# Two graph layers on one core: PSUM banks of the first layer grouped by the engine that empties them

## The chip, the cores and the metric

The kernel runs on one core of one Trainium2 chip. The metric is device time in microseconds (us): the median of repeated executions. Before the change it is 2896.18 us (three runs, 2895.3 to 2902.11).

The engines are called here as the profile calls them: PE (TensorE, matrix products), PEld (its weight loads), DVE (VectorE), ACT (ScalarE), POOL (GpSimd), SP (SyncE, which starts transfers). PE writes its results into PSUM, eight banks of 512 fp32 values per partition. DVE or ACT takes a result up into the ordinary on-chip memory, and only then can PE fill that bank anew. Emptying a bank in this way is called taking it up.

## The reference, cut to what matters

Inputs are 16 graphs of 1024 nodes with 128 features each (`x`), a weighted adjacency `adj` of 16 x 1024 x 1024, and a node mask.

```python
# layer 0: three steps per graph
h = jnp.maximum(_layernorm(x), 0.0)
for i in range(3):
    h = h @ W[i] + b[i]
    nh = h / jnp.maximum(jnp.linalg.norm(h, axis=-1, keepdims=True), EPS)
    ew = edge_weight * jnp.einsum('bij,bkj->bik', nh, nh)
    h = jnp.einsum('bpq,bqc->bpc', ew, h)          # relu between steps
x = x + h

# layer 1
h = jnp.maximum(_layernorm(x), 0.0)
adj_d = adj * dilate(adj > 0, mask)                # row by row; each row's removals act on later rows
for i in (1, 2, 3):
    agg = adj_d @ h / clip(sum(adj_d), 1)
    h_i = batchnorm(relu(normalize(agg @ Wr + h @ Wx + b)))
x = x + (concat(h_1, h_2, h_3) @ Wl + bl)
```

`dilate` depends on `adj` and the mask alone, not on the features. The kernel can therefore work on it while layer 0 runs.

## The kernel before, in words

The program has two stages. The first (lines 169 to 775) holds layer 0 for all 16 graphs and, interleaved with it, the dilation. The second (from line 778) holds layer 1. The change touches the first stage only.

**Layer 0.** A graph's 1024 x 1024 matrix is treated as 8 x 8 blocks of 128 x 128. The cosine matrix is symmetric, so only the block rows q with their 8 - q blocks from the diagonal on are multiplied. Per graph and step (48 in all), and per block row, the methods of `Batch` do this:

- `products` (L296): PE multiplies up to four blocks at a time into a bank `pg` (L311). DVE multiplies it by the adjacency and writes both the block and the one that mirrors it into `ew` (L320 the diagonal block, L323 the others).
- `turn` (L331): the mirrored blocks are transposed by PE into a bank `gt` (L340), and ACT copies them back into `ew` (L341).
- `sums` (L343) and `sums_back` (L359): PE adds the blocks times the features into `po`, two banks that stay open for the whole step (L351, L365). At the end ACT takes `po` up as `hTo` (L374).
- `features` (L252), `turned` (L274), `scaled` (L280): the next step's features go through a bank `pw` (L260), which DVE takes up (L264 or L270). They are normalized and transposed through `pt_n` (helper `transposed`, L165 and L166, taken up by ACT).
- `adjT_tile` (L216): blocks of the adjacency are transposed through banks `pt_a` (L227), taken up by ACT (L228). `enter` transposes the entering features (`pt_h`). `residual` turns the result back through `px` (L385), taken up by DVE (L388).

`layer0` (L406) writes these steps out by hand as a generator. A block row's `sums` follow its `products` by three block rows (`LAG = 3`), the transposes come in between, and each `yield` returns a weight.

**Dilation.** `dilation` goes through 8 row blocks in two halves of 8 graphs each. For each graph it loads adjacency rows (`an`, L535) and kept entries (`kl`, L541), and ACT makes the pattern (`patt`, L537 and L538). PE then transposes it and makes thresholds (`pdt` L559, `pT` L566 to L568, both taken up by ACT). A few rounds follow, in which PE counts into a bank `pc` (L622, L623) and DVE computes the next estimate (L639, L593, L613, L617). A last transpose goes through `pe` (L671), taken up by ACT (L672). Then DVE scans each graph's rows (L689), ACT takes absolute values (L698), DVE compares (L709) and POOL stores (L710).

The loop at L744 advances layer 0 by the returned weights so that the two works go forward side by side. The dilation gets through when layer 0 has done 93% of its share (`SPREAD = 0.93`). After it comes a branch (L769) that holds an exact second dilation, which is run only if the quick one did not settle.

**Who sets the order.** The tile framework orders the instructions of each engine when the program is built. It goes by program order as priority, by the data, and by when a buffer of the right pool is free. On the chip each engine carries its own list out in that order. A tile gets a bank out of its pool's fixed number, so the number and the mixture of tiles in a pool enter into the order as well as into the waits.

The PSUM pools before are `a_sm` (2 banks: `pt_a`, `pt_h`, `pt_n`, `pw`, `px`, `pdt`, `pT`, `pc`, `pe`, `mt`, `pf`), `a_g` (2 banks: `pg`), `a_o` (`po`, one tile of 2 banks) and `a_t` (2 banks: `gt`).

Of the kernel before, what the change touches and what calls it, by code (L numbers as in the profile page):

```python
# [8 lines left out]
F32 = mybir.dt.float32  # L9
# [7 lines left out]
P = 128  # L17
# [29 lines left out]
def tile_adj_preln_d2(  # L47
# [112 lines left out]
    def transposed(psum_pool, dst, src, nm, func=AF.Copy, halves=range(NHALF)):  # L160

        for h in halves:
            pt = psum_pool.tile([P, CPH, P], F32, tag="sm", name=f"pt_{nm}_{h}")
            for c in range(CPH):
                nc.tensor.transpose(pt[:, c, :], src[:, h * CPH + c, :], ident)  # L165
            nc.scalar.activation(dst[:, h * CPH : (h + 1) * CPH, :], pt, func)  # L166


    with ExitStack() as actx:
        pool1 = actx.enter_context(tc.tile_pool(name="a1", bufs=1))  # L170
        pool2 = actx.enter_context(tc.tile_pool(name="a2", bufs=2))
        ps_sm = actx.enter_context(tc.tile_pool(name="a_sm", bufs=2, space=PSUM))
        ps_g = actx.enter_context(tc.tile_pool(name="a_g", bufs=2, space=PSUM))
        ps_o = actx.enter_context(tc.tile_pool(name="a_o", bufs=1, space=PSUM))
        ps_t = actx.enter_context(tc.tile_pool(name="a_t", bufs=2, space=PSUM))

        w0 = pool1.tile([P, 3, P], F32, name="w0")
        b0 = pool1.tile([P, 3, P], F32, name="b0")
# [37 lines left out]
        def adjT_tile(b, q):  # L216

            place, nat, row = adj_place(b, q), Nat.pop((b, q)), NCH - q
            if row > 1:
                nc.sync.dma_start(  # L220
                    place[:, row:, :].rearrange("p c q -> p (c q)"), adj[b][q * P : (q + 1) * P, (q + 1) * P :]
                )
            for c in range(0, row, CPH):
                n = min(CPH, row - c)
                pt = ps_sm.tile([P, CPH, P], F32, tag="sm", name=f"pt_a{b}_{q}_{c}")
                for i in range(n):
                    nc.tensor.transpose(pt[:, i, :], nat[:, c + i, :], ident)  # L227
                nc.scalar.activation(place[:, c : c + n, :], pt[:, :n, :], AF.Copy)  # L228
            nc.gpsimd.dma_start(adjT_d[b][q][:, q * P :], place[:, :row, :].rearrange("p c q -> p (c q)"))

        class Batch:
# [15 lines left out]
            def enter(self, h):  # L247
                if h == 0:
                    self.hT = pool2.tile([P, NCH, P], F32, tag="hT", name=f"hT_{self.b}")
                transposed(ps_sm, self.hT, self.h, f"h{self.b}", halves=(h,))  # L250

            def features(self, h):  # L252

                nm, l, rn = f"{self.b}_{self.l}", self.l, self.rn
                if h == 0:
                    self.hN = pool1.tile([P, NCH, D], F32, tag="hN", bufs=1, name=f"hN_{nm}")
                hc = slice(h * CPH, (h + 1) * CPH)
                pw = ps_sm.tile([P, CPH, P], F32, tag="sm", name=f"pw_{nm}_{h}")
                for c in range(CPH):
                    nc.tensor.matmul(  # L260
                        pw[:, c, :], lhsT=self.hT[:, h * CPH + c, :], rhs=w0[:, l, :], start=True, stop=True
                    )
                if rn is None:
                    nc.vector.tensor_tensor(  # L264
                        self.hN[:, hc, :], pw, b0[:, l : l + 1, :].to_broadcast([P, CPH, P]), ALU.add
                    )
                else:
                    for c in range(CPH):
                        n = h * CPH + c
                        nc.vector.scalar_tensor_tensor(  # L270
                            self.hN[:, n, :], pw[:, c, :], rn[:, n : n + 1], b0[:, l, :], ALU.mult, ALU.add
                        )

            def turned(self):  # L274

                nhT = pool1.tile([P, NCH, P], F32, tag="nhT", bufs=2, name=f"nhT_{self.b}_{self.l}")
                transposed(ps_sm, nhT, self.hN, f"n{self.b}_{self.l}")
                self.next_nhT = nhT.rearrange("p c q -> p (c q)")

            def scaled(self):  # L280
# [15 lines left out]
            def products(self, s):  # L296

                q = SEQ[s]  # L300
                nm = f"{self.b}_{self.l}_{q}"
                row = NCH - q

                most = max(NCH - SEQ[s % 4], NCH - SEQ[s % 4 + 4])
                ew = pool1.tile([P, 2 * most - 1, P], F32, tag=f"ew{s % 4}", name=f"ew_{nm}")
                place = adj_place(self.b, q)
                both = [t[:, 1 : 2 * row - 1, :].rearrange("p (t c) q -> p t c q", t=2) for t in (ew, place)] if row > 1 else None
                for c in range(0, row, CPH):
                    n = min(CPH, row - c)
                    pg = ps_g.tile([P, CPH, P], F32, tag="pg", name=f"pg_{nm}_{c}")  # L310
                    nc.tensor.matmul(  # L311
                        pg[:, :n, :].rearrange("p c q -> p (c q)"),
                        lhsT=self.nhT[:, q * P : (q + 1) * P],
                        rhs=self.nhT[:, (q + c) * P : (q + c + n) * P],
                        start=True,
                        stop=True,
                    )
                    own = c == 0
                    if own:
                        nc.vector.tensor_tensor(ew[:, 0, :], pg[:, 0, :], place[:, 0, :], ALU.mult)  # L320
                    if n > own:
                        off = slice(c + own - 1, c + n - 1)
                        nc.vector.tensor_tensor(  # L323
                            both[0][:, :, off, :],
                            pg[:, own:n, :].unsqueeze(1).to_broadcast([P, 2, n - own, P]),
                            both[1][:, :, off, :],
                            ALU.mult,
                        )
                return (ew,)

            def turn(self, s, ew):  # L331

                q = SEQ[s]
                row = NCH - q
                for c in range(1, row, CPH):
                    n = min(CPH, row - c)
                    pt = ps_t.tile([P, CPH, P], F32, tag="gt", name=f"gt_{self.b}_{self.l}_{q}_{c}")
                    at = row + c - 1
                    for i in range(n):
                        nc.tensor.transpose(pt[:, i, :], ew[:, at + i, :], ident)  # L340
                    nc.scalar.activation(ew[:, at : at + n, :], pt[:, :n, :], AF.Copy)  # L341
# [37 lines left out]
            def residual(self):  # L379
                b = self.b  # L380
                self.x2 = x2 = pool2.tile([P, NCH, D], F32, tag="tt", name=f"x2_{b}")
                for h in range(NHALF):
                    pt = ps_sm.tile([P, CPH, P], F32, tag="sm", name=f"px_{b}_{h}")
                    for c in range(CPH):
                        nc.tensor.transpose(pt[:, c, :], self.hT[:, h * CPH + c, :], ident)  # L385
                    for c in range(CPH):
                        n = h * CPH + c
                        nc.vector.scalar_tensor_tensor(  # L388
                            x2[:, n, :], pt[:, c, :], self.rn[:, n : n + 1], self.xb[:, n, :], ALU.mult, ALU.add
                        )  # L390
                nc.gpsimd.dma_start(x2_d[b].rearrange("(c p) d -> p c d", p=P), x2)
# [125 lines left out]
        def dilate(k, half, exact):  # L517
# [14 lines left out]
            for i in range(BH):  # L532
# [21 lines left out]
                if i % GT == GT - 1:  # L554
                    four = range(i - GT + 1, i + 1)
                    bs_ = slice(i - GT + 1, i + 1)
                    pdt = ps_sm.tile([P, GT, P], F16, tag="sm", name=f"pdt{nk}_{i}")
                    for n, ii in enumerate(four):
                        nc.tensor.transpose(pdt[:, n, :], pattern(ii)[:, diag], ident16)  # L559
                    dT = pool2.tile([P, GT, P], F16, tag="dT", bufs=1, name=f"dT{nk}_{i}")  # L560
                    nc.scalar.activation(dT, pdt, AF.Copy)
                    nc.vector.tensor_scalar(rbias[:, bs_], rest[:, bs_], 2.0, -2.0, ALU.mult, ALU.add)
                    yield 0.1
                    pT = ps_sm.tile([P, GT, P], F32, tag="sm", name=f"pT{nk}_{i}")
                    for n, ii in enumerate(four):
                        nc.tensor.matmul(pT[:, n, :], lhsT=dT[:, n, :], rhs=upto, start=True, stop=False)  # L566
                        nc.tensor.matmul(pT[:, n, :], lhsT=pattern(ii)[:, diag], rhs=off, start=False, stop=False)
# [28 lines left out]
            def removals(x, nm):  # L596
# [13 lines left out]
                else:  # L610
# [4 lines left out]
                        nc.vector.tensor_tensor(ev, ev, x, ALU.is_gt)  # L615
                        nc.vector.scalar_tensor_tensor(par, x, 1.0, ev, ALU.is_gt, ALU.mult)
                    nc.vector.tensor_tensor(E, T, mid.unsqueeze(2).to_broadcast([P, BH, P]), ALU.is_equal)  # L617
                pc = ps_sm.tile([P, BH], F32, tag="sm", name=f"pc_{nm}")
                for i in range(BH):
                    c = pc[:, i : i + 1]  # L620
                    if ends:
# [44 lines left out]
            if ends:  # L666
                nc.vector.tensor_tensor(Z, Z, par.unsqueeze(2).to_broadcast([P, BH, P]), ALU.mult)
                nc.vector.tensor_tensor(E, E, Z, ALU.add)
            pe_ = ps_sm.tile([P, BH, P], F16, tag="sm", name=f"pe{nk}")
            for i in range(BH):  # L670
                nc.tensor.transpose(pe_[:, i, :], E[:, i, :], ident16)  # L671
            nc.scalar.activation(E, pe_, AF.Copy)  # L672
# [59 lines left out]
        nc.gpsimd.dma_start(mi, nodemask.rearrange("b (c p) -> (b c) p", p=P))  # L732
        mfl = pool1.tile([P, P], F32, tag="up", name="mfl")[:NB, :]
        nc.vector.tensor_copy(mfl, mi)
        mt = ps_sm.tile([P, NB], F32, tag="sm", name="mt")
        nc.tensor.transpose(mt, mfl, ident[:NB, :NB])
        mf_flat = mf.rearrange("p b c -> p (b c)")
        nc.vector.tensor_copy(mf_flat, mt)
# [7 lines left out]
            while at * total < done * SPREAD * total0 and step0():  # L746
                pass

        pf = ps_sm.tile([1, B // 2], F32, tag="sm", name="pf")
        nc.tensor.matmul(pf, lhsT=ones_col, rhs=astray, start=True, stop=True)  # L750
        off_f = pool1.tile([1, 1], F32, name="off_f")
        nc.vector.tensor_reduce(off_f, pf, mybir.AxisListType.X, ALU.add)
# [382 lines left out]
```

## Time and profile before

| what | us |
|---|---|
| median of three runs | 2896.18 |
| the profiled execution, its own time | 2901.99 |
| its span from first to last instruction | 2900.3 |
| mean granted PE clock | 0.978 |
| PE busy in the span | 2667.8 |
| DVE busy | 1937.8 |
| ACT busy | 1426.8 |
| POOL busy | 467.5 |
| last dilation compare on DVE (L709) starts | 1578.3 |
| last `pg` product of layer 0 (L311) starts | 1694.9 |

The profile comes from one execution. Its own time is 5.8 us above the median of the runs. "Busy" counts a matmul from its start to its modelled end, and matmuls overlap, so a row of products shows as busy without a gap even though each of them takes up PE's entrance for less time than its own duration.

### The profile page before, as it was taken

To read this page: it belongs to the slowest core of one execution; us is meant where nothing else is said; L and a number is where in the kernel's file an instruction comes from. 1 tells how busy PE (TensorE), PEld (TensorE's weight loads), DVE (VectorE), ACT (ScalarE), POOL (GpSimd) and SP (SyncE) were. 2 spreads that over 40 slices of the span, in tenths; PEclk is the share of its full clock that TensorE was granted. 3 is DMA by queue.
4 is the path that set the end of the run, shared out by engine and by line. 5 is a ranking of instruction groups with operands and counts; after the bars stand their busy time and mean duration, and the time that the engine had idled before them with its cause. 6 is when DMAs were issued, how large, how long until landed. Compare 5 with 4: busy or idle time off the path is not lost. (4 is left out here: it accounts for less than half of the span.)

```text
span 2900.3 us, 52009 instructions
## 1 busy us (share of the span) xinstructions
PE 2667.8 (92%) x18803; PEld 2203.2 (76%) x18803; DVE 1937.8 (67%) x4913; ACT 1426.8 (49%) x4100; POOL 467.5 (16%) x619
## 2 busy tenths in 40 slices
PE   6999999899999998988999979999989999899997
PEld 4666676666666666666676758988979999899996
DVE  3787778877878788779877447777772232355565
ACT  6767667557556566455455323333333333333334
POOL 3111112011111111021011002222220010010101
PEclk9999999999999999999999989999999999999999
DMA  9446357347355475296162049999995656566764
GB/s 282 138 142 215 87 173 238 88 143 209 102 178 166 111 231 158 72 258 188 40 190 96 1 154 409 405 403 387 405 371 174 210 199 208 182 228 231 235 226 136
DMA packets 382236, 585.24 MB, mean 202 GB/s; under 512 B 85201, under 2 KB 266449, under 8 KB 381969
## 3 DMA queue, kind: packets, MB, share of 16 engines
q1 hardware_dynamic: 343280, 425.28, 46.4%
q0 software_dynamic: 38688, 156.53, 14.5%
q8 instruction: 152, 2.49, 0.3%
q14 instruction: 116, 0.94, 0.1%
HBM read 403.44 MB, written 163.58 MB: 196 GB/s over the span
## 5 line engine op out<-in xcount | busy, mean ns | idle before, releaser
L832 PE MATMUL agg<-hw,aT 128*128 128x128 f32 (+1 forms) x6144 | 744.8, 277 | 8.6 <-DVE aT L942 7.3
L832 PEld LDWEIGHTS agg<-hw,aT 128*128 128x128 f32 x6144 | 713.5, 193 | 14.3 <-DVE aT L942 9.7
L311 PE MATMUL pg<-nhT 128*128 128x512 f32 (+3 forms) x1152 | 454.0, 497 | 71.4 <-DVE ew L323 61.3
L351 PE MATMUL po<-ew,hS 128*128 128x512 f32 (+3 forms) x1152 | 455.5, 499 | 8.4 <-ACT hTo L374 4.3
L323 DVE TENSOR_TENSOR ew<-pg,adjA 128x768 f32<-128x768 f32 (+3 forms) x528 | 423.4, 824 | 3.7 <-DVEq L769 3.2
L365 PE MATMUL po<-ew,hS 128*128 128x128 f32 x2688 | 368.2, 277 | 0.0
L365 PEld LDWEIGHTS po<-ew,hS 128*128 128x128 f32 x2688 | 339.8, 193 | 35.5 <-issue 34.0
L341 ACT ACTIVATE ew<-gt 128x512 f32<-128x512 f32 (+1 forms) x480 | 208.7, 465 | 266.8 <-PE gt L340 262.7
L311 PEld LDWEIGHTS pg<-nhT 128*128 128x128 f32 x1152 | 188.8, 192 | 174.2 <-issue 131.3
L689 DVE TENSOR_TENSOR_SCAN rank<-patt 128x1024 f16<-128x1024 f16 x128 | 293.0, 2294 | 0.8
L351 PEld LDWEIGHTS po<-ew,hS 128*128 128x128 f32 x1152 | 195.7, 194 | 99.2 <-issue 68.7
L340 PEld LDWEIGHTS gt<-ident,ew 128*128 128x128 f32 x1344 | 169.6, 144 | 97.9 <-issue 71.1
L320 DVE TENSOR_TENSOR ew<-pg,adjA 128x128 f32<-128x128 f32 x384 | 107.2, 279 | 183.0 <-PE pg L311 143.2
L340 PE MATMUL gt<-ident,ew 128*128 128x128 f32 x1344 | 213.2, 278 | 3.5 <-ACT ew L341 3.2
L882 POOL TENSOR_TENSOR o<-o,rn 128x512 f32<-128x512 f32 x96 | 107.2, 1116 | 651.3 <-DVE rn L881 632.5
L804 PE MATMUL pw<-wrx,hT 128*128 128x256 f32 x768 | 182.4, 392 | 10.4 <-ACT hT L1007 9.7
L806 DVE TENSOR_TENSOR own<-pw,bs 128x256 f32<-128x256 f32 x192 | 81.3, 423 | 152.2 <-ACT hw L805 152.2
L804 PEld LDWEIGHTS pw<-wrx,hT 128*128 128x128 f32 x768 | 147.0, 197 | 33.5 <-ACT hT L1007 10.5
L960 ACT ACTIVATE aT<-pta 128x512 f32<-128x512 f32 (+3 forms) x160 | 71.2, 466 | 203.1 <-PE pta L959 172.2
L861 DVE SCALAR_TENSOR_TENSOR o<-agg,invdeg,own 128x128 f32<-128x128 f32 x384 | 109.7, 344 | 87.1 <-PE agg L832 78.4
L877 ACT ACTIVATE own<-o 128x128 f32<-128x128 f32 x384 | 114.6, 301 | 106.7 <-DVE o L861 106.7
L288 POOL TENSOR_TENSOR hS<-hN,rn 128x1024 f32<-128x1024 f32 x48 | 94.9, 1978 | 398.8 <-DVE rn L157 299.5
(165 smaller groups left out, 3950.1 us busy)
## 6 DMA issues: line engine op xcount, KB each, us to landing
an<-in_adj_dram SPq DMA_DIRECT2D x128, 512.0 KB, 4.7
keep<-kp POOLq DMA_DIRECT2D x128, 256.0 KB, 4.0
kb<-keep SPq DMA_DIRECT2D x128, 256.0 KB, 5.6
aT<-adT SPq DMA_DIRECT2D x32, 960.0 KB, 5.2
aT<-adT SPq DMA_DIRECT2D x32, 832.0 KB, 5.0
aT<-adT SPq DMA_DIRECT2D x32, 704.0 KB, 4.8
aT<-adT SPq DMA_DIRECT2D x32, 576.0 KB, 3.4
xb<-in_x_dram SPq DMA_DIRECT2D x31, 512.0 KB, 4.8
```

The lines of the kernel that those rows point to most:

```text
L311: nc.tensor.matmul(pg[:, :n, :].rearrange("p c q -> p (c q)"), lhsT=self.nhT[:, q * P : (q + 1) * P], rhs=self.nhT[:, (q + c) * P : (q + c ...
L320: nc.vector.tensor_tensor(ew[:, 0, :], pg[:, 0, :], place[:, 0, :], ALU.mult)
L323: nc.vector.tensor_tensor(both[0][:, :, off, :], pg[:, own:n, :].unsqueeze(1).to_broadcast([P, 2, n - own, P]), both[1][:, :, off, :], ALU ...
L340: nc.tensor.transpose(pt[:, i, :], ew[:, at + i, :], ident)
L341: nc.scalar.activation(ew[:, at : at + n, :], pt[:, :n, :], AF.Copy)
L351: nc.tensor.matmul(self.po[:, c * P : (c + n) * P], lhsT=self.hS[:, q, :], rhs=ew[:, c - q : c - q + n, :].rearrange("p c q -> p (c q)"), ...
L365: nc.tensor.matmul(self.po[:, q * P : (q + 1) * P], lhsT=self.hS[:, q + n, :], rhs=ew[:, NCH - 1 - q + n, :], start=False, stop=closes and ...
L689: nc.vector.tensor_tensor_scan(rank, pt[:, 1 : N + 1], pt[:, 2:], 0.0, ALU.add, ALU.add)
L804: nc.tensor.matmul(pw[:, i, :], lhsT=hT[:, 2 * h + i, :], rhs=wrx[:, l, :], start=True, stop=True)
L832: nc.tensor.matmul(self.place(c), lhsT=aT[:, blk, :], rhs=self.hw[:, source, :], start=source == 0 and c % self.ga == 0, stop=ends(c, source),
L861: nc.vector.scalar_tensor_tensor(self.o[:, c, :], self.place(c)[:, :P], invdeg[:, b, c : c + 1], self.own[:, c, :], ALU.mult, ALU.add,)
L877: nc.scalar.activation(self.own[:, n, :], self.o[:, n, :], AF.Square, accum_out=ss[:, c : c + 1])
```

## The change

Two pools of the first stage, `a_sm` and `a_t`, go away as such, and `a_g` too. In their place stand `a_v` with three banks for all tiles that DVE takes up (`pg`, `pw`, `px`, `pc`, `mt`, `pf`) and `a_s` with three banks for all tiles that ACT takes up (`pt_a`, `pt_h`, `pt_n`, `gt`, `pdt`, `pT`, `pe`). `po` keeps its two. No instruction is added or removed, and no size changes. All eight banks are in use before and after.

```diff
-        ps_sm = actx.enter_context(tc.tile_pool(name="a_sm", bufs=2, space=PSUM))
-        ps_g = actx.enter_context(tc.tile_pool(name="a_g", bufs=2, space=PSUM))
+
+        ps_v = actx.enter_context(tc.tile_pool(name="a_v", bufs=3, space=PSUM))
+        ps_s = actx.enter_context(tc.tile_pool(name="a_s", bufs=3, space=PSUM))
         ps_o = actx.enter_context(tc.tile_pool(name="a_o", bufs=1, space=PSUM))
-        ps_t = actx.enter_context(tc.tile_pool(name="a_t", bufs=2, space=PSUM))
...
-                pt = ps_sm.tile([P, CPH, P], F32, tag="sm", name=f"pt_a{b}_{q}_{c}")
+                pt = ps_s.tile([P, CPH, P], F32, tag="sm", name=f"pt_a{b}_{q}_{c}")
...
-                transposed(ps_sm, self.hT, self.h, f"h{self.b}", halves=(h,))
+                transposed(ps_s, self.hT, self.h, f"h{self.b}", halves=(h,))
...
-                pw = ps_sm.tile([P, CPH, P], F32, tag="sm", name=f"pw_{nm}_{h}")
+                pw = ps_v.tile([P, CPH, P], F32, tag="sm", name=f"pw_{nm}_{h}")
...
-                transposed(ps_sm, nhT, self.hN, f"n{self.b}_{self.l}")
+                transposed(ps_s, nhT, self.hN, f"n{self.b}_{self.l}")
...
-                    pg = ps_g.tile([P, CPH, P], F32, tag="pg", name=f"pg_{nm}_{c}")
+                    pg = ps_v.tile([P, CPH, P], F32, tag="sm", name=f"pg_{nm}_{c}")
...
-                    pt = ps_t.tile([P, CPH, P], F32, tag="gt", name=f"gt_{self.b}_{self.l}_{q}_{c}")
+                    pt = ps_s.tile([P, CPH, P], F32, tag="sm", name=f"gt_{self.b}_{self.l}_{q}_{c}")
...
-                    pt = ps_sm.tile([P, CPH, P], F32, tag="sm", name=f"px_{b}_{h}")
+                    pt = ps_v.tile([P, CPH, P], F32, tag="sm", name=f"px_{b}_{h}")
```

In the same way `pdt`, `pT` and `pe` go to `ps_s`, and `pc`, `mt` and `pf` to `ps_v`.

More of the change, by code (lines that the diff above doesn't have):

```diff
@@ L556, in dilate @@
                     bs_ = slice(i - GT + 1, i + 1)
-                    pdt = ps_sm.tile([P, GT, P], F16, tag="sm", name=f"pdt{nk}_{i}")
+                    pdt = ps_s.tile([P, GT, P], F16, tag="sm", name=f"pdt{nk}_{i}")
                     for n, ii in enumerate(four):
@@ L563, in dilate @@
                     yield 0.1
-                    pT = ps_sm.tile([P, GT, P], F32, tag="sm", name=f"pT{nk}_{i}")
+                    pT = ps_s.tile([P, GT, P], F32, tag="sm", name=f"pT{nk}_{i}")
                     for n, ii in enumerate(four):
@@ L617, in removals @@
                     nc.vector.tensor_tensor(E, T, mid.unsqueeze(2).to_broadcast([P, BH, P]), ALU.is_equal)
-                pc = ps_sm.tile([P, BH], F32, tag="sm", name=f"pc_{nm}")
+                pc = ps_v.tile([P, BH], F32, tag="sm", name=f"pc_{nm}")
                 for i in range(BH):
@@ L668, in dilate @@
                 nc.vector.tensor_tensor(E, E, Z, ALU.add)
-            pe_ = ps_sm.tile([P, BH, P], F16, tag="sm", name=f"pe{nk}")
+            pe_ = ps_s.tile([P, BH, P], F16, tag="sm", name=f"pe{nk}")
             for i in range(BH):
@@ L734, in tile_adj_preln_d2 @@
         nc.vector.tensor_copy(mfl, mi)
-        mt = ps_sm.tile([P, NB], F32, tag="sm", name="mt")
+        mt = ps_v.tile([P, NB], F32, tag="sm", name="mt")
         nc.tensor.transpose(mt, mfl, ident[:NB, :NB])
@@ L747, in tile_adj_preln_d2 @@
                 pass
-        pf = ps_sm.tile([1, B // 2], F32, tag="sm", name="pf")
+        pf = ps_v.tile([1, B // 2], F32, tag="sm", name="pf")
         nc.tensor.matmul(pf, lhsT=ones_col, rhs=astray, start=True, stop=True)
```

## The prediction, made before the result was known

> **What bounds the kernel now.** I read the busy shares first, then the same cut at the end of the dilation, since a whole-span share mixes two stages. The last dilation compare starts at 1578 us and the last product of layer 0 at 1695 us. Columns: length of the stretch, then busy us (instructions) of PE, PEld, DVE, ACT, POOL, then granted clock and DMA.
>
> ```profile
> PE 2667.8 (92%) x18803; PEld 2203.2 (76%) x18803; DVE 1937.8 (67%) x4913; ACT 1426.8 (49%) x4100; POOL 467.5 (16%) x619
> ...
> 150.00:1580.00 1430.00, 1311.36 (x8276) 955.40 (x8275) 1144.88 (x2714) 848.75 (x2274) 232.19 (x300) 0.99 0.53 156
> 1580.00:1704.00 124.00, 119.93 (x673) 86.77 (x671) 55.31 (x142) 39.29 (x117) 9.42 (x6) 1.00 0.04 12
> ```
>
> While the dilation runs beside layer 0 (first row), PE is busy for 92%, DVE for 80%, ACT for 59%. Once it has ended (second row), PE runs at 97%. So PE sets the length of the first stage, and what it loses it loses while DVE and ACT have the dilation to do as well. The next view is PE's waits from 0 to 1580 us: what waited, for whom, us in total, times, longest.
>
> ```profile
> PE pg L311 <- DVE ew L323: 60.0, 41, 3.6
> PE pt_a L227 <- DMA nat<-in_adj_dram: 21.4, 11, 7.0
> PE pc L623 <- DVE E L617: 11.0, 12, 2.2
> PE pg L311 <- DVE rn L157: 7.2, 4, 2.8
> PE po L351 <- ACT hTo L374: 4.3, 6, 1.5
> PE px L385 <- ACT adjA L228: 4.0, 2, 2.7
> ...
> PE pt_h L165 <- DVE x L388: 3.7, 5, 1.0
> ...
> PE gt L340 <- ACT ew L341: 3.2, 2, 2.9
> ```
>
> A `pg` product reads only `nhT`, which ACT writes. Its wait for DVE (first row) is therefore a wait for a bank that DVE hasn't emptied. In the same way `px` waits for a bank that ACT empties and `pt_h` for one that DVE empties: the mixed pool ties the two engines together. `gt` with its own two banks hardly waits.
>
> Busy time understates the loss, since a product counts for about 0.17 us after PE could have taken the next. This row shows it: 14 products in 1.73 us.
>
> ```profile
> 1680.15 1.73 PE L365 MATMUL po<-ew,hS 128*128 128x128 f32 x14
> ```
>
> Less one duration (0.277), 13 steps take 1.45 us, or 0.11 us for 128 columns. I therefore took, from the trace's start times from 0 to 1704 us, each start less the start before and less that step. Losses over 0.1 us sum to 214 us. Where the product is the first into its bank and starts within 0.35 us of the end of the bank's last reader, I count it as a wait for a bank. `pg`: 80.7 us in 60 places. The tiles of the mixed pool: 40.3 (`pt_a` 9.2, `pw` 8.9, `pt_n` 8.7, `pt_h` 5.8, `px` 4.7, `pdt` 2.1, `pc` 0.9). `po`: 10.9. `gt`: 3.5. Together 135 of the 214 us.
>
> **What the Trainium skill says.** "PSUM — Partial Sum Buffer", section "PSUM bank collisions raise a hardware error": two engines must not be in one bank at once, so waits go by the bank, not the address. The trace agrees: `pg` starts no earlier than 0.06 us after the last reader's end. "TensorE: Matmul & The Clock Gate", section "Architectural detail": ACT and DVE take their queues strictly in order, and PE pulls only weight loads ahead. So one late tile on DVE delays all behind it, and one product without a bank stops PE. The trace agrees: DVE sits in the dilation's 2.29 us scan while PE waits. "Perfetto Trace Analysis", section "Optimization Strategy": repeated gaps on the engine that should be full can mean too few PSUM tiles. The 60 `pg` waits fit that.
>
> **The change part by part.** All eight banks are used before and after, and no instruction is added. I compared the two built orders. Layer 1 is in the same order. In the first stage the two works advance at the same pace (each dilation half stands within 10 us of PE work of its old place), and the swaps are local. For each tile I added up the PE work, by the steps above, between the last product into a bank and the next tile's first. That is the cover under which the bank must be emptied.
>
> (a) *`pg` gets three banks, shared.* Of some 575 fills, those with cover under 3 us fall from 190 to 135; the lower quartile rises from 2.47 to 3.23 us. Take 0.8 us off each of the 60 waits: 39 us go. Not all stays. At these places DVE was 3 us or more late with other work, and the transposes of the same `ew` follow some 3.5 us of PE work later (median in the order). I let 40% come back there: -24 us. Bounds: 0 (DVE is late anyway) and -81 (all waits go).
>
> (b) *No more mixing.* `px`, `pw`, `pt_h` (19.4 us) no longer meet a foreign engine. Fills with cover under 1 us fall from 6 to 0, 16 to 2 and 7 to 2, so I let all 19.4 go. `pt_a`, `pt_n`, `pdt`, `pc` (20.9 us): `pt_a` under 1 us falls from 26 to 12, `pt_n` under 2 us from 38 to 22, so 40% go, 8.4. A quarter of the 27.8 comes back at the next wait: -21 us. Bounds 0 and -40.
>
> (c) *`gt` loses its own banks* and queues with `pt_a` and the dilation. Fills with cover under 2 us rise from 0 to 31 of 480. ACT needs 0.59 us for a full `gt` and may be behind. I take 0.2 us each, +6. Bounds: +1 (its own time alone) and +60, the second rival. A gain is excluded beyond the 3.5 us it loses now.
>
> (d) *Step boundaries.* `po` keeps its banks, but the order puts less work ahead of the next step's first sum. Nine of 47 have under 1 us, where three had; ACT's `hTo` alone takes 1.02 us. With 1.38 us needed from last product to first, the shortfalls sum to 15.5 us instead of 9.4: +6. Bounds 0 and +12.
>
> (e) *Dilation rounds.* Between one round's last `pc` product and the next's first, PE has 2.27 us of other work on the mean instead of 2.86, since the rounds stand closer. DVE's own work in between, in its order, falls as well, from 1.99 to 1.69. With 0.3 us for the two hand-overs the shortfalls go from 1.5 to 8.9 us: +7. Bounds 0 and +15.
>
> (f) *The branch at L769* stands 4 us of PE work ahead of the last sum's end instead of 14. PE lost 1.2 us at it, which stays, and 1.3 us just after, waiting for DVE's `ew`; no `pg` is left behind it now: -1 (0 to -4).
>
> DMAs: none added, and the SP order of layer 1 is unchanged. In the first stage a load moves by at most 10 of 515 places in SP's queue, a store by 2 of 368 in POOL's. DMA is busy 53% there, so I cost this at nothing. If that cover is gone, the 21 us of `pt_a` waits on loads grow.
>
> Sum: -24 - 21 + 6 + 6 + 7 - 1 = -27 us. Against the profiled execution's own 2902 us that is 2875; it stands 6 us above the median, so 2869 from the median of 2896.
>
> **The rivals.**
>
> *Full gain.* Bank waits go and hardly any time comes back: (a) -39, (b) -40, the rest +18, sum -61: 2835. For it: DVE is at 80%, so it has time to catch up, and only 45 of the 166 us lost between 150 and 1580 us lie in 10 us windows with DVE at 95% or more. Against it: every freed us brings the next reader of a late tile nearer.
>
> *The gain meets DVE.* PE runs ahead, then stops at `gt` or `pc` for data in place of a bank: (a) and (b) leave -20 and the rest takes 18, near -2: 2894. For it: at the stalled `pg` DVE has been full for the 5 us before and nearly so for 10 us after. Against it: the gaps of DVE that wait for `pg` (114.5 us up to 1580) show that it is short of work elsewhere.
>
> *Slower: ACT stops and all its banks fill.* ACT works in order and waits for the dilation's loads and scans:
>
> ```profile
> ACT patt L537 <- DMA an<-in_adj_dram: 67.2, 35, 6.0
> ACT patt L537 <- DVE rank L689: 62.8, 47, 3.7
> ```
>
> These are 82 stops, 130 us. Tiles for ACT come at 880 in about 1600 us, one per 1.8 us. Before, `gt` had two banks that no stop of `pt_a` could fill, beside the mixed pool's two; now all share three. If the lost bank exposes PE for 1.8 us at a third of the 82 stops, that is +49, and with -27 it makes +22: 2918. It decides once bank waits of ACT's tiles exceed the 29 us of now (`pt_a`, `pt_h`, `pt_n`, `pdt`, `gt`) by over some 30 us. Against it: stops average 1.6 us, and three banks are about 5 us of tiles.
>
> **How the numbers follow.** Forecast (2846 to 2887) 0.45, full gain 0.14, meets DVE 0.18, slower 0.23. The measurement tells about 0.3%, 9 us, from no change, so the bounds are 2887 and 2905. Meets DVE (2880 to 2905) falls mostly between them: faster 0.62, same 0.15, slower 0.23. The range leaves out half of the full gain below 2836 and something over half of the slower case above 2912: some 0.2.
>
> **What would show it.** (a) `pg` waits for DVE down from 60 us to about half. (b) No `px` or `pt_h` waiting for the other engine's tile. (c) `gt` waits for `ew` L341 below 12 us; above 40, the slower rival is right. (d), (e) `po` waits for `hTo` and `pc` for `E` up by some 6 us each. PE busy in the dilation's stretch up from 92% to about 94%. Layer 1 unchanged in length, within 3 us. If `gt` or `po` waits for data of DVE take over the `pg` time, the third case holds.

## The result, and the profile after

The changed kernel takes 2924.9 us (median of 4 runs, 2920.7 to 2926.2) beside 2895.7 for the kernel before (with a fourth run beside the three above): ratio 1.0096, 95% interval 1.008 to 1.0112. It is slower by about 29 us; the forecast was 27 us faster, and the range ended at 2912.

First the engines' busy times of the whole span of the changed kernel, from its page.

```profile
PE 2676.7 (92%) x18803; PEld 2204.1 (75%) x18803; DVE 1937.2 (66%) x4913; ACT 1423.9 (49%) x4100; POOL 473.6 (16%) x619
```

Then the two stretches that the prediction used (stretch, its length, busy us and instructions of PE, PEld, DVE, ACT, POOL, granted clock, DMA share, GB/s). The profile lists an fp32 product as two, a transpose as one.

```profile
150.00:1580.00 1430.00, 1295.28 (x8092) 938.85 (x8091) 1123.15 (x2674) 826.72 (x2219) 230.99 (x292) 0.98 0.53 155
1580.00:1704.00 124.00, 122.92 (x696) 89.57 (x695) 65.33 (x140) 49.29 (x150) 13.76 (x13) 1.00 0.06 21
```

The work is the same, instruction for instruction. In the first stretch PE got through 8092 entries where it had done 8276, DVE through 2674 instructions for 2714, ACT through 2219 for 2274: all three fell behind together, by about 2%. PE was busy for 91% of it, where 94% was forecast. The last dilation compare starts at 1608 us for 1578. Layer 1, from its first transpose to the end, takes 1184.6 us for 1189.8. So the whole loss, and 5 us more, lies in the first stage.

PE's waits from 0 to 1600 us in the changed kernel (who waited for whom, us in total, times, longest):

```profile
PE gt L340 <- DVE ew L323: 40.6, 54, 2.6
PE pg L311 <- DVE ew L323: 24.4, 16, 4.0
PE pt_a L227 <- DMA nat<-in_adj_dram: 19.8, 11, 7.0
PE po L351 <- ACT hTo L374: 16.1, 18, 4.0
PE pc L623 <- DVE E L617: 13.6, 17, 2.6
PE pg L311 <- DVE x L388: 7.6, 6, 2.1
PE pt_n L165 <- ACT ew L341: 5.0, 7, 1.1
PE pdt L559 <- ACT patt L538: 5.0, 2, 4.4
```

In the kernel before the wait of the first row came to 0.3 us (the last figure of this line, which covers the whole span):

```profile
L340 PE MATMUL gt<-ident,ew 128*128 128x128 f32 x1344 | 213.2, 278 | 3.5 <-ACT ew L341 3.2 <-DVE ew L323 0.3
```

`gt`'s bank is emptied by ACT, so a `gt` that waits for DVE waits for data, the product `ew`. The row that led before, `pg` for `ew`, has fallen from 60.0 us to 24.4. `po`'s wait for `hTo` has gone from 4.3 to 16.1. And `pg` now waits for `x` as well (7.6 us), which is what DVE makes of `px`: the two share banks.

I repeat the count of the prediction (each product's start less the one before and its step, losses over 0.1 us, a bank wait where the product starts within 0.35 us of the last reader's end). PE lost 214 us in the first stage before; it now loses 245. By tile, before and after, in us:

| tile, reason | before | after |
|---|---|---|
| `pg`, bank | 80.7 | 41.4 |
| `gt`, data | 10.7 | 60.3 |
| `po`, bank and data | 23.0 | 40.6 |
| `pc`, data | 16.3 | 24.6 |
| `pw`, `px`, `pt_h`, bank | 19.4 | 6.3 |
| `pt_a`, `pt_n`, `pdt`, `gt`, bank | 23.5 | 18.1 |
| `pw`, `pt_n`, `pdt`, data | 7.1 | 19.0 |

Not all of this is waiting. PE's granted clock stands at 0.5 in short stretches of the first stage, 61 us in all before and 85 in the changed kernel, where 13 of the 15 stretches begin within 2 us of the end of a PE wait of 2 us or more. Of the losses counted, 27 us before and 41 after lie in such stretches, so up to 14 of the 31 us may be slower products that follow a wait. The clock isn't what starts the loss: `row1_pg_pc_pw` (below) loses 27 us in the count with 68 us of such stretches and 30 us of losses in them.

### The profile page after: what moved, and what is told of

The parts are those of the page before. It is cut to its first block, busy times and chain, and to the rows that moved or that the text cites. A ratio compares the mean times of both kernels' runs of the same rounds, so it can differ in the third digit from the quotient of the medians.

```text
span 2924.4 us, 52051 instructions
## 1 busy us (share of the span) xinstructions
PE 2676.7 (92%) x18803; PEld 2204.1 (75%) x18803; DVE 1937.2 (66%) x4913; ACT 1423.9 (49%) x4100; POOL 473.6 (16%) x619
## 5 line engine op out<-in xcount | busy, mean ns | idle before, releaser
L311 PE MATMUL pg<-nhT 128*128 128x512 f32 (+3 forms) x1152 | 456.6, 503 | 35.8 <-DVE ew L323 24.4
L351 PE MATMUL po<-ew,hS 128*128 128x512 f32 (+3 forms) x1152 | 452.6, 499 | 19.8 <-ACT hTo L374 16.1
L340 PEld LDWEIGHTS gt<-ident,ew 128*128 128x128 f32 x1344 | 163.7, 143 | 159.3 <-issue 76.5
L340 PE MATMUL gt<-ident,ew 128*128 128x128 f32 x1344 | 215.8, 278 | 44.8 <-DVE ew L323 40.6
L537 ACT ACTIVATE patt<-an 128x1024 f16<-128x1024 f32 (+7 forms) x128 | 87.4, 685 | 175.5 <-DVE rank L689 96.7
```

The costliest lines, as they stand in the source:

```text
L311: nc.tensor.matmul(pg[:, :n, :].rearrange("p c q -> p (c q)"), lhsT=self.nhT[:, q * P : (q + 1) * P], rhs=self.nhT[:, (q + c) * P : (q + c ...
L351: nc.tensor.matmul(self.po[:, c * P : (c + n) * P], lhsT=self.hS[:, q, :], rhs=ew[:, c - q : c - q + n, :].rearrange("p c q -> p (c q)"), ...
```

## The experiments

Three theories stood at the start. *Same late tile*: a third bank can't help, because the `pg` that waits for a bank and the `gt` that waits for `ew` wait for the same late DVE instruction. *Shared ScalarE banks*: `gt` queues for banks with all other tiles of ACT. *Order*: the new order costs time at step boundaries and dilation rounds. Later came *theory G* (the features queue behind `pg`'s late banks), *theory O* (any new order may cost some 10 us by chance, a redraw), *grouping* (putting all of DVE's tiles in one pool costs something by itself) and *theory R*, a sharper form of *order*: the pools decide what `pg` may overtake when PE's list is built. Lists are built before the run, and a pool's tiles take its banks in turn; what stands in PE's list is then done in that order.

For the last one I use a number from the built lists, not from a trace: the PE work of layer 0 that stands ahead of a `pg` in the program but behind it in PE's list, as a mean over all `pg` ("overtaken" below). "Past `pc`" is the same for the dilation's `pc`, which the first number leaves out, as a sum over all `pg`. All runs at a glance; "loss" is PE's loss in the first stage, counted as above, and "time" the difference from the kernel before in the same session, whose median was 2896 to 2899 us:

| run | overtaken us | past `pc` us | loss us | time us |
|---|---|---|---|---|
| kernel before | 0.32 | 41 | 214 | 0 |
| changed kernel | 0.08 | 0 | 245 | +29 |
| `unmixed_222` | 0.05 | 0 | 244 | +31 |
| `pg_three` | 0.52 | 51 | 217 | +9 |
| `turn_late_before` | 0.49 | 41 | 232 | +19 |
| `turn_late_after` | 0.21 | 1 | 282 | +69 |
| `after_pw_s` | 0.17 | 0 | 246 | +35 |
| `after_pc_s` | 0.25 | 43 | 238 | +21 |
| `before_s92` | 0.36 | 39 | 217 | +7 |
| `after_s92` | 0.06 | 2 | 240 | +32 |
| `before_pc_g` | 0.16 | 0 | 244 | +31 |
| `before_pw_g` | 0.11 | 34 | 233 | +18 |
| `pure_pg_213` | 0.37 | 47 | 225 | +7 |
| `pg_two_four` | 0.41 | 47 | 237 | +21 |
| `row1_pg_pc` | 0.18 | 0 | 248 | +34 |
| `row1_pg_pc_pw` | 0.12 | 0 | 241 | +34 |
| `pure_pg_222` | 0.43 | 48 | 225 | +22 |

### The change in halves: the grouping alone, and the third bank alone

`unmixed_222` groups by engine with the old numbers of banks; `gt` keeps its own two.

```diff
-ps_v = ... "a_v", bufs=3      # of the changed kernel
-ps_s = ... "a_s", bufs=3
+ps_v = ... "a_v", bufs=2
+ps_s = ... "a_s", bufs=2
+ps_t = ... "a_t", bufs=2      # gt
```

> Grouping alone, no third bank and gt by itself: two banks for all VectorE tiles (pg, pw, px, pc), two for all ScalarE tiles but gt, two for gt. Theory 'same late tile': pg waits for a bank again (80 us or more, since pw, px and pc share its two), gt no longer waits for ew (under 20 us), time 2895 to 2910. Rival 'shared ScalarE banks': with gt apart the loss goes, 2895 or below. Rival 'order': between 2900 and 2925 with losses at po and pc as in the changed kernel.

2927.8 us, ratio 1.0092 (1.006 to 1.0123). No third bank, `gt` apart, and still the full loss, though it lies elsewhere: `pg` bank 79 us, `pw` bank 24, `gt` data 14. The first two theories missed the time; *order*, 2900 to 2925, came within 3 us. So the grouping is enough to lose 29 us, and `gt` without banks of its own isn't needed for it.

`pg_three` gives `pg` three banks of its own and mixes the rest, `gt` too, in three.

```diff
-"a_sm", bufs=2; "a_g", bufs=2; "a_t", bufs=2   # of the kernel before
+"a_sm", bufs=3; "a_g", bufs=3                  # gt takes from a_sm
```

> The third bank alone: pg has three banks of its own, everything else, gt included, shares the other three as a mixed pool. Theory 'same late tile': bank waits at pg fall to 40 us or less and waits of gt for ew rise to 50 us or more as in the changed kernel; no gain, 2905 to 2930. If pg's third bank were a gain that the grouping spoils, this would be 2880 or less. Rival 'shared ScalarE banks': slower than the changed kernel, 2930 or more, with the waits at gt for banks and not for ew.

2905.8 us, ratio 1.0028 (1.0016 to 1.004). PE's waits from 0 to 1600 us in this kernel:

```profile
PE gt L340 <- DVE ew L323: 43.4, 57, 3.1
PE pt_a L227 <- DMA nat<-in_adj_dram: 23.7, 10, 6.9
PE pc L623 <- DVE E L617: 19.0, 19, 3.6
PE pc L622 <- DVE par L616: 10.1, 4, 3.8
PE po L351 <- ACT hTo L374: 6.3, 9, 1.4
```

No `pg` row is left. In the count `pg`'s bank wait went from 81 us to none, and `gt`'s data wait from 11 to 58, `pc`'s from 16 to 35: 214 us of loss became 217.

`pg_two_four` is the same with one bank moved back: `pg` two, everything else mixed in four.

> `pg` with its two banks as before, all other tiles, `gt` among them, mixed in four. Theory R: 2890 to 2906 (PE work that a `pg` overtakes: 0.41 us); the `pg` bank waits stay near 80 us and `gt` data waits near 11, since both meet the same late DVE instruction and only a third bank for `pg` moves the wait on. If `gt` needs banks of its own: 2910 or more, with bank waits of ACT's tiles up by 10 us and more.

2918.2 us, ratio 1.007 (1.0048 to 1.0093): a miss, it was expected at 2890 to 2906. As expected, `pg` waits 84 us for a bank and `gt` only 16 for data (PE's waits from 0 to 1600 us):

```profile
PE pg L311 <- DVE ew L323: 68.2, 53, 3.7
PE pt_a L227 <- DMA nat<-in_adj_dram: 25.9, 10, 7.0
PE pc L623 <- DVE E L617: 20.8, 20, 3.6
```

Between these two kernels only the place of one bank differs, and the order that follows from it. In `pg_three` it takes away 84 us of bank waits at `pg`; 42 us come back as `gt`'s data waits, and 39 at the banks of `pt_a`, `pt_h`, `pt_n` and `gt`, which have one fewer; other waits shrink by 17. PE's loss falls by 20 us, the time by 12. That is what a third bank for `pg`, taken from the mixed four, was worth; *same late tile* describes half of the wait (42 of 84 us). And merging `gt`'s two banks with the mixed two cost 21 us, though bank waits of ACT's tiles did not rise: `pc` waits for data 34 us for 16, and `pt_n`, `po`, `gt` and `pt_a` by 5 to 9 more each. I can't say by which path.

### Taking the new wait away

In both kernels `turn`, which issues `gt`, comes one row later, so that DVE has longer for `ew`.

```diff
-if s > 0 and now or s == 0 and i:
-    b_, *of = behind[-2 if now else -1]
-    if now or s == 0:
-        b_.turn(*of)
-        yield (NCH - 1 - SEQ[of[0]]) * TURN
+if len(behind) > 2 and now or not now and s < 2:
+    b_, *of = behind[-3 if now else s - 2 if s == 0 else -1]
+    b_.turn(*of)
+    yield (NCH - 1 - SEQ[of[0]]) * TURN
```

> The changed kernel with the transposes of each block row put one block row later in the hand-written order, so that some 3.5 us more PE work lie between the pg products and the transposes that read their ew. Theory 'same late tile': the wait of pg for a bank and the wait of gt for ew end with the same DVE instruction, so the third bank only moved the wait to gt (losses ahead of gt rose from 14 to 63 us in the trace). With the transposes later these fall from 63 us to under 20 and the time falls by 35 to 45 us, to about 2880 to 2890, below the kernel before. Rival 'shared ScalarE banks': gt suffers because it queues for banks with all other ScalarE tiles; then putting it later leaves 2920 within 10 us. Rival 'order': the loss lies in step boundaries and dilation rounds; then 2910 or more.

> The same edit on the kernel before. Theory 'same late tile': here PE stops at pg for the bank (81 us) and the transposes hardly wait (14 us), so the edit can gain 10 us at most: 2885 to 2900. If it gains as much as on the changed kernel (35 us or more), the gain there says nothing of the third bank.

`turn_late_after` takes 2966.1 us (ratio to the kernel before 1.0217, 1.0184 to 1.025), `turn_late_before` 2916.1 us (1.0058, 1.0043 to 1.0073); *same late tile* missed both. In the changed kernel `gt`'s data waits fell from 60 to 8 us, as meant, and the others rose by more: `po` for data from 18 to 43, `pc` from 25 to 47, `pt_a` for a bank from 8 to 25. Taking the new wait away didn't take the loss away. As the edit costs 19 us in the kernel before too, this run alone can't show that the wait isn't the cause; `unmixed_222` does, which has the full loss with 14 us of it.

### Which tile must not share?

`after_pw_s` moves `pw` and `px` of the changed kernel from DVE's pool to ACT's, `after_pc_s` moves `pc`. Beside them the pace of the two works is redrawn in both kernels (`SPREAD` 0.92 for 0.93).

```diff
-pw = ps_v.tile(...)   # after_pw_s, px likewise; after_pc_s: pc
+pw = ps_s.tile(...)
```

> The changed kernel with `pw` and `px` moved from DVE's pool to ACT's: DVE's three banks then hold `pg` and `pc` alone. Theory G (putting the features and the turned `hT` behind `pg`'s late banks makes each step's start late): 2900 to 2912, the `pw` and `po` waits back near those of before, the last dilation compare ending near 1590 us instead of 1608. Theory O (the new pools merely redraw the built order, and any redraw may cost or gain some 10 us): no tie to what was moved, 2905 to 2940. If `pc` is what costs: no change from the 2925 of the changed kernel.

> The changed kernel with `pc` alone moved from DVE's pool to ACT's: the dilation's rounds no longer wait behind `pg` for a bank. If `pc` sharing with `pg` is what slows the dilation (and with it the whole first stage, since both works advance together): 2895 to 2910, the `pc` and `E` part of the waits down by some 10 us. Theory G on the features: no change, 2920 to 2930. Theory O: anywhere from 2905 to 2940.

> The kernel before with the pace of layer 0 against the dilation at 0.92 instead of 0.93: about one per cent of layer 0's work is issued later, which redraws the local order everywhere and changes no pool. Theory O: moves by 10 us or more either way without a reason that could have been told ahead. Theories that tie the 29 us to the pools: within 6 us of the kernel before (2891 to 2903).

> The same redraw on the changed kernel. Theory O: 2900 to 2945, so that its distance from the redrawn kernel before is no longer about 29 us. Theories that tie the 29 us to the pools: the distance from the redrawn kernel before stays 20 to 35 us.

In this order: 2932.5 us (ratio 1.012, 1.0086 to 1.0155), 2918.8 (1.0093, 1.0057 to 1.0128), 2904.2 (1.0023, 1.0012 to 1.0033), 2930.1 (1.0126, 1.0089 to 1.0162). Theory G and the forecast for `pc` both missed: neither tile alone brings the time back, though taking `pc` away gives 8 of the 29 us. The redraw moves the kernel before by 7 us and the changed one by 3, and leaves 26 us between them: this redraw of the order is worth 3 to 7 us, not 29. It isn't a small one: to turn the list before into the redrawn one, 1710 of its 7917 product and transpose instructions must change place, and only 603 in the first run of "The order alone" below, which costs 34 us. `after_pw_s` gave the clue. Beside `pg_three` it differs in `pc`'s pool (and that of `mt` and `pf`, used once each), and it is 26 us slower.

So I moved one kind of tile in the kernel before, into `pg`'s two banks, and took `pg` out of the changed kernel's pool.

```diff
-pc = ps_sm.tile(..., tag="sm")   # before_pc_g; before_pw_g: pw and px
+pc = ps_g.tile(..., tag="pg")
```

```diff
-pg = ps_v.tile(...)   # pure_pg_213: a_g 2, a_v 1, a_s 3; pure_pg_222: 2, 2, 2
+pg = ps_g.tile(...)
```

> The kernel before with one tile moved: `pc` takes its bank from `pg`'s two instead of the mixed pool's two; no third bank, `gt` stays apart. Theory R (a `pg` that has its banks to itself can be issued ahead of late work when the order is built; one that shares them with anything is tied to the program's order, and the stage loses some 25 us): 2912 to 2928, since in its built order the PE work that a `pg` overtakes falls from 0.32 us on the mean to 0.16. Theory 'engine-pure grouping costs' (all of DVE's tiles in one pool): less than half of it, 2896 to 2908. If only the number of banks counts: 2893 to 2900.

> The kernel before with `pw` and `px` moved to `pg`'s two banks, `pc` left in the mixed pool. Theory R: 2912 to 2930 (PE work that a `pg` overtakes: 0.11 us on the mean). If `pc` is what must not share: 2893 to 2900. If only the number of banks counts: 2893 to 2900.

> The changed kernel's grouping by engine kept, but `pg` by itself: two banks for `pg`, one for DVE's other tiles (`pw`, `px`, `pc`), three for all of ACT's, `gt` among them. Theory R: the loss of the changed kernel is gone, 2890 to 2906, although no tile of ACT shares with one of DVE and `gt` has no banks of its own (PE work that a `pg` overtakes: 0.37 us). The single bank of `pw` may cost: it comes in pairs, some 48 pairs of up to 0.6 us, which would add up to 29 us and end at 2925; the row of `pw` waits tells. Theory 'engine-pure grouping costs': 2920 to 2930.

> The changed kernel's grouping by engine with `pg` by itself: two banks for `pg`, two for DVE's other tiles, two for all of ACT's (PE work that a `pg` overtakes: 0.43 us). If a `pg` with its own banks is what counts: 2890 to 2910, with bank waits of ACT's tiles some 10 us above those with three banks. If all of ACT's tiles need three banks: 2915 or more. It also tells whether a better split than that of the kernel before is near: below 2890.

`before_pc_g` 2927.8 us (ratio 1.0106, 1.008 to 1.0131); `before_pw_g` 2915.1 (1.006, 1.0039 to 1.008); `pure_pg_213` 2904.7 (1.0022, 1.0008 to 1.0036); `pure_pg_222` 2920.7 (1.0079, 1.006 to 1.0097), a miss of its first expectation and a hit of its second: ACT's tiles, `gt` among them, want three banks; the third is worth some 15 us, though DVE's other tiles give it up. In the count their bank waits are 60 us with two banks and 21 with three, though PE's loss in all is the same 225 us in the two profiled executions. `pc` takes a bank 62 times in the main path, `pg` 576 times; letting the 62 share costs as much as the whole change. Taking `pg` out again gives back 22 of the 29 us with all else still grouped by engine. So the grouping by engine costs some 7 us in this split; what costs is sharing with `pg`.

### The order alone

The last two runs leave the pools as before. A tie, which only binds the built list (PE's then holds 1933 semaphore waits for 1920, so next to none is added), puts each `pg` behind the `pc` ahead of it in the program and each `pc` behind the `pg` ahead of it; the second run ties `pw` too.

```diff
+def tied(first, last):
+    if len(row_of) > 0:
+        tc.add_manual_dep(first, row_of[-1].name,
+            mybir.DependencyInfo(mybir.DependencyClass.NoSync, mybir.DependencyReason.DATA), reason="row")
+    row_of.append(last)
...
+                    tied(mm.ins, mm.ins)      # after each pg
...
+                if not exact:
+                    tied(mm[0], mm[-1])       # after each pc
```

> The kernel before with its pools untouched, but each `pg` tied in PE's order behind the `pc` that the program has before it, and each `pc` behind the `pg` before it. Only the built order changes (PE work that a `pg` overtakes: 0.18 us for 0.32, as in the run where `pc` shares `pg`'s banks, 0.16); no bank is shared that wasn't. If the order is the cause: 2912 to 2930, near the 2928 of that run. If the shared banks themselves are (a product that waits on the chip for the other tile's reader): 2893 to 2903.

> The same tie for `pg`, `pc` and `pw` (PE work that a `pg` overtakes: 0.12 us; 0.08 in the changed kernel). If the order is the cause: 2915 to 2935. If the shared banks are: 2893 to 2903.

2932.8 us (ratio 1.0119, 1.0099 to 1.0139) and 2932.5 (1.0124, 1.0104 to 1.0144), the first 3 us above what *order* forecast, the second inside. No pool has gained or lost a bank or a tile, and the whole loss is there. This also settles a rival not named so far: the changed kernel's list makes PE wait for 2270 semaphores instead of 1920, but `row1_pg_pc` has the loss with 1933, and `pure_pg_213` loses 7 us with 2237. PE's waits in `row1_pg_pc` from 0 to 1600 us (its lines stand 9 or 10 further down):

```profile
PE pg L320 <- DVE ew L333: 63.9, 51, 4.2
PE pt_a L236 <- DMA nat<-in_adj_dram: 22.1, 10, 7.0
PE pc L634 <- DVE E L627: 14.5, 17, 3.6
PE po L361 <- ACT hTo L384: 9.3, 12, 1.5
PE pw L269 <- ACT hT L166: 5.3, 3, 2.5
PE pc L633 <- DVE par L626: 4.9, 4, 2.1
```

The `pg` row is that of before (60.0); what grew is spread thin: in the count `pc` for data from 16 to 26 us, `po` from 23 to 29, `pt_a` for a bank from 9 to 15, `gt` for data from 11 to 15, `pt_h` for a bank from 6 to 10, and a dozen rows by 1 to 3 us.

One place shows what the tie takes away. PE in time order (start, us, line, what, count, and the idle time with its releaser), first the kernel before:

```profile
909.37 1.08 PE L311 MATMUL pg<-nhT 128*128 128x512 f32 x2
...
910.98 1.08 PE L311 MATMUL pg<-nhT 128*128 128x512 f32 x2
...
912.54 0.49 PE L340 MATMUL gt<-ident,ew 128*128 128x128 f32 x3
...
913.31 0.39 PE L311 MATMUL pg<-nhT 128*128 128x128 f32 x2
...
914.62 0.27 PE L340 MATMUL gt<-ident,ew 128*128 128x128 f32 x1
915.64 0.35 PE L623 MATMUL pc<-one,E 128*128 128x1 f16 x8 [0.75 <-DVE E L617]
```

Then the same `pc` (dilation 4, second half, first round) in the changed kernel:

```profile
931.43 1.05 PE L365 MATMUL po<-ew,hS 128*128 128x128 f32 x8
935.04 0.36 PE L623 MATMUL pc<-one,E 128*128 128x1 f16 x8 [2.55 <-DVE E L617]
935.26 2.05 PE L311 MATMUL pg<-nhT 128*128 128x512 f32 x2
```

Before, the first three `pg` of the next step (two entries each) stand ahead of a `pc` whose `E` isn't ready; they fill the time, and DVE has their banks to work on early. In the changed kernel the first of them stands right behind `pc`, and PE waits 2.55 us instead of 0.75, with a `pg` behind that then starts at once. That `pg` takes 2.05 us where it took 1.08, for here the granted clock is at 0.5 (the figure behind POOL's):

```profile
935.10:938.50 3.40, 3.40 (x12) 1.65 (x13) 2.87 (x6) 0.26 (x1) 0.00 (x0) 0.50 0.50 151
```

In `row1_pg_pc` the wait here is 1.44 us:

```profile
937.16 0.35 PE L634 MATMUL pc<-one,E 128*128 128x1 f16 x8 [1.44 <-DVE E L627]
937.37 0.64 PE L236 MATMUL pt_a<-ident,nat 128*128 128x128 f32 x4
937.85 1.45 PE L320 MATMUL pg<-nhT 128*128 128x512 f32 x3
```

Over the stage `pg` overtook 61 us of PE work of `pw`, 41 of `pc`, 37 of `pt_a` and 32 of `pt_h` in the kernel before; in the changed one none of `pw` and `pc`, and 11 of `pt_a`.

The column "past `pc`" parts the runs in two. In all nine kernels that lose at most 22 us, the kernel before among them, `pg` overtakes 34 to 51 us of `pc`; in all eight that lose 29 or more, at most 2. "Overtaken" doesn't part them so (`before_pw_g` has 0.11 us and +18, `row1_pg_pc` 0.18 and +34). This was seen after the runs, and a tie of `pg` against `pw` alone was not run.

## Why the prediction was wrong

**What failed.** The sentence "the two works advance at the same pace ... and the swaps are local". Both halves hold in the built lists, and I took from them that the new order costs only what two covers show, (d) and (e), +13 us. An order of this kind costs 34 us by itself (`row1_pg_pc`, `row1_pg_pc_pw`), and 18 or 31 where one kind of tile shares `pg`'s two banks (`before_pw_g`, `before_pc_g`). I compared where each tile stood against its old place and how much PE work lay between two uses of a bank. I did not ask what a tile was free to overtake. A pool of its own had let `pg` be put ahead of late work; in a shared pool it goes in turn with `pw` and `pc`. Term by term, as worked out below, the trace gives +11, -6, -1, +18 and +8, 30 of the 31 us that PE lost. By size (a) is furthest off, by 35 us; but `unmixed_222`, whose `pg` waits 79 us for banks as before, loses as much, so (a) is where the loss shows and not what makes it.

**(a), -24.** The bank wait fell by 39 us, as forecast (80.7 to 41.4). What came back at `gt` was 50 us, not 40% of 39, so (a) ends at +11. "The same `ew` follow some 3.5 us of PE work later" was in the working, and is the point: a late DVE instruction that delays a bank delays data a moment later too. Alone, a third bank was worth 12 us (`pg_two_four` to `pg_three`). The Trainium skill ("Perfetto Trace Analysis", "Optimization Strategy") says that repeated gaps can mean too few PSUM tiles; here 66 such gaps did go with one bank more, and only one seventh of their 84 us was gained.

**(b), -21.** `px` and `pt_h` no longer meet the other engine, and `pw`, `px`, `pt_h` lost 13 us of bank waits of the 19.4 forecast, the other tiles of the mixed pool about 5. But `pw`, `pt_n` and `pdt` wait 12 us longer for data. Some -6 is left.

**(c), +6.** In the changed kernel `gt`'s own bank waits did not rise (3.5 to 2.8 us), so nothing shows here. Other splits show that its banks matter by more than 6 us: merged with the mixed pool +21, with all of ACT's in two banks +22, in three +7 (each with what else that kernel changes).

**(d), +6, and (e), +7.** The direction was right. `po` lost 18 us more, three times the forecast, `pc` 8 more.

**(f)** and layer 1. From the last dilation compare to the last `pg` it is 116 us before and 112 after, in which the 1 us of (f) can't be told. Layer 1 is 5 us shorter, where within 3 was forecast; why stays open.

**The rivals.** "Slower" named ACT's banks as its mechanism, deciding once bank waits of ACT's tiles exceeded 29 us by over 30. They fell, to 22 us. So it had the sign and, by 7 us, the time, with the wrong cause. "The gain meets DVE" described (a) rightly, PE stopping at `gt` for data, and ended at 2894, since it too had no price for the order.

**What stays open.** The terms don't add up tile by tile: `pc` alone shared costs 31 us, `pw` and `px` alone 18, all of them 29 to 31. The ties also move other tiles, and DVE's and ACT's lists with PE's, so the runs show that a built order makes a loss of this size by itself, not that each lost us is a `pg` that could have overtaken. "Overtaken" doesn't order the kernels by itself; 0.41 and 0.43 us go with +21 and +22, where `gt`'s banks seem to be a second cost. The old order on the new pools would be the direct proof; it wasn't tried on the chip. No split tried beats the kernel before, and none of the runs points to one.

## What to carry to other kernels

Where lists are built before the run, a pool is also a queue: tiles that take banks in turn are tied to the program's order, so give the tile that fills gaps (here `pg`) banks that nothing late shares. A wait for a bank is worth its removal only if the engine that empties the bank isn't also the one whose data is needed next: look for the next reader of the same late instruction before counting the gain. When a built order changes, list what each tile overtakes before and after, not only how far it moved.

## What the runs showed that I had not expected

Losses move more than they go: in the first stage `gt`'s data wait fell by 53 us (`turn_late_after`) while the total rose by 37, and `pg`'s bank wait fell by 81 (`pg_three`) while the total rose by 3. PE's total loss, on the other hand, followed the measured time: in fourteen of the sixteen other kernels its change is within 6 us of the time's, in `row1_pg_pc_pw` 7, in `pure_pg_222` 11, where the profiled execution was 8 us below the median.
